# A two-layer graph kernel: gathers issued two blocks ahead with GpSimd's own arithmetic between them, and the first and last loads rearranged

## The chip, the cores and the metric

The kernel runs on one core of a Trainium2 chip. The metric is the time of one execution in device microseconds, as the median of several runs; less is better. Profiles come from one further execution, recorded instruction by instruction.

## The reference

There are 4096 nodes with 512 features each, and an adjacency matrix of 4096 x 4096 int32 values of which about one in a thousand is 1, so a node has some four neighbours. Layer 0 is an eight-head graph attention with a residual and a layer norm; layer 1 takes the mean over the neighbours, two linear maps and a combining one, a relu, a residual and a layer norm.

```python
Wh   = einsum('nf,hfo->hno', x, W)                       # 8 heads of 64
e    = leaky_relu(f1[:, :, None] + f2[:, None, :], 0.2)  # f1, f2: Wh times the halves of a
attn = softmax(where(adj > 0, e, -9e15))
x    = layernorm(x + concat_heads(attn @ Wh))

agg  = (adj > 0) @ x / max(deg, 1)
out  = concat(x @ W_self + b_self, agg @ W_nb + b_nb) @ W_comb + b_comb
x    = layernorm(x + relu(out))
```

## The kernel before

The 4096 rows are handled as 32 blocks of 128. Since the matrix is sparse, the kernel makes lists of neighbours from it and gathers rows instead of multiplying with it. (A dense version stands behind a flag and is not run with these inputs.) The order of instructions on each engine is the order in which the code is written: the schedule is by hand. There are five stages.

**Start.** The weights come in. `fold_weights(1, ...)` multiplies `W_nb` with its half of `W_comb` into `m2` (L265 to L278 and L283), so that layer 1 needs one product per block; VectorE folds the attention vector into `w_sb` (L690, L695). `mask_adj` is a relu on ScalarE (L364) that turns a half block of adjacency into bf16, counts it, and frees its load buffer, of which there are four (`at`).

**Adjacency.** For each block: x is transposed on PE (L301), multiplied with `w_sb` (L309), and the resulting row written to a table `t0` in HBM (L723, the last one L736). `fold_adj`, `max_keys` and, for every four blocks, the generator `decode` turn the adjacency into lists: `idx` holds five row numbers per node, three of its own and two shared slots for nodes with more neighbours, and `es` says to whom the shared ones belong. x is loaded eight blocks ahead and adjacency two blocks ahead on SP's queue.

**First turn.** `gather` (L494) takes the rows of a block with five indirect DMAs issued from GpSimd, into one of `GA = 5` buffers `g`. The first four blocks are gathered at once, twenty DMAs in a row. Meanwhile `fold_weights(0, ...)` makes `m1` from `W_self`, and `split_bias` turns the folded bias into three bf16 rows (`b3`) on VectorE (L251 to L256).

**Attention.** A pipeline over the blocks, one step per block. The softmax of block i+2 (L518 to L549) and the weighting of block i+1 (L562) are on VectorE, the sums over rows on PE (L569, L572, L576), the layer norm of block i on VectorE with its root on GpSimd (`a_moments`, L594), and block i-1 is multiplied with `m2` (L604) and written to the table `t1` (L609). One gather of five DMAs is issued per step, four blocks ahead, after the root.

**Second turn and layer 1.** When `t1` is complete, its rows are gathered in the same way: four blocks at once, and then per block after `g_moments`, when a buffer is free. `g_self` (L620, L623) multiplies a block of x with `m1` and adds the bias; `g_shared` (L627) adds the shared rows on PE; `g_adds` (L614, L615) adds the own ones on VectorE; `g_moments` (L634 to L641) joins them and takes the moments; the square root is on ScalarE (L643) and its reciprocal on VectorE (L646); `g_norm` writes the result (L648, L650, L651).

The order around the second turn, before:

```python
        if i >= NB - 1 and i - NB + 1 < 2:
            g_self(i - NB + 1, transposed(i - NB + 1, wp, "key"), m1)
    G1 = {b: gather(t1, b, gp) for b in range(GA - 1)}
```

Of the kernel before, what the change touches and what calls it, by code (L numbers as in the profile page):

```python
# [39 lines left out]
P = 128  # L40
# [44 lines left out]
def listed_layers(  # L85
# [107 lines left out]
    nc.vector.memset(mhalf, -0.5)  # L193
    eps = const.tile([P, 1], F32, name="eps")
    nc.vector.memset(eps, EPS)
    oner = const.tile([1, P], F32, name="oner")
    nc.vector.memset(oner, 1.0)
    inv_n = const.tile([P, 1], F32, name="inv_n")
    nc.vector.memset(inv_n, 1.0 / N)

# [16 lines left out]
    b3 = const.tile([3, HD], BF16, name="b3")  # L217
    brow = const.tile([1, HD], F32, name="brow")

    tmp_cm.__exit__(None, None, None)  # L220
# [11 lines left out]
    def load_fold(k, w, fp):  # L232
        wr = fp.tile([P, FB, HD], F32, name="wr")
        nc.sync.dma_start(wr, w.rearrange("(c p) o -> p c o", p=P))
        wc = fp.tile([P, FB, HD], F32, name="wc")
        nc.sync.dma_start(
            wc, w_comb[k * HD : (k + 1) * HD, :].rearrange("(c p) o -> p c o", p=P)
        )
        return wr, wc

    def load_bias(k, wp):
        bcol = wp.tile([P, FB], F32, name="bcol", bufs=1)
        with nc.allow_non_contiguous_dma(reason="a vector of 512"):
            nc.scalar.dma_start(bcol, (b_self, b_nb)[k].rearrange("(c p) -> p c", p=P))
        return bcol

    def split_bias(wp):

        bc = wp.tile([P, HD], F32, name="y", bufs=2)[0:1, :]
        nc.scalar.dma_start(bc, b_comb.rearrange("(a o) -> a o", a=1))  # L250
        nc.vector.tensor_add(brow, brow, bc)  # L251
        for k in range(3):
            bb = wp.tile([P, KH * P], F32, name="own", bufs=4)[0:1, :].bitcast(BF16)
            nc.vector.tensor_copy(bb, brow)
            nc.vector.tensor_sub(brow, brow, bb)
            nc.scalar.dma_start(b3[k : k + 1, :], bb)  # L256

    def fold_weights(k, loaded, bcol, m, wp, last=None):

# [11 lines left out]
        for c in range(FB):  # L271
# [8 lines left out]
            yield  # L280
        bp = ps.tile([1, HD], F32, name="nm", bufs=2)
        for d in range(FB):
            nc.tensor.matmul(  # L283
                bp, lhsT=bcol[:, d : d + 1], rhs=wc[:, d, :], start=(d == 0), stop=(d == FB - 1)
            )
        if k == 0:
            nc.vector.tensor_add(brow, brow, bp)
        else:
            nc.vector.tensor_copy(brow, bp)

# [101 lines left out]
    def decode(b0, dp, wp):  # L392
# [46 lines left out]

        sts = []  # L440
        for b in range(b0, b0 + G):
            lt = wp.tile([P, KH * P], F32, name="st", bufs=2)
            nc.vector.tensor_scalar(lt, iota[:, 0 : KH * P], end[:, b : b + 1], None, OP.is_lt)  # L443
            st = wp.tile([P, KH * P], F32, name="own", bufs=4)
            nc.vector.scalar_tensor_tensor(
                st, iota[:, 0 : KH * P], lst[:, b, KL : KL + 1], lt, OP.is_ge, OP.mult
            )
            sts.append(st)
# [41 lines left out]

    def gather(table, b, gp):
        g = gp.tile([P, KS, TW], F32, name="g")
        for k in range(KS):
            nc.gpsimd.indirect_dma_start(  # L494
                out=g[:, k, 0 : table.shape[1]],
                out_offset=None,
                in_=table[:, :],
                in_offset=bass.IndirectOffsetOnAxis(ap=idx[:, b, k : k + 1], axis=0),
            )
        return g  # L500
# [4 lines left out]
    def a_owners(b, wp):  # L505
        OWN[b] = owners(b, wp)
# [74 lines left out]
    def a_two(b, wp):  # L581
        Y[b] = wp.tile([P, HD], F32, name="y", bufs=2)
        nc.vector.tensor_add(Y[b], G0[b][:, 0, H:TW], G0[b][:, 1, H:TW])

# [47 lines left out]
    def g_moments(b):  # L632
# [9 lines left out]
        RS[b] = small.tile([P, 1], F32, name="ln_rs")  # L642
        nc.scalar.activation(RS[b], MV[b][:, 1:2], AF.Sqrt, bias=eps)  # L643

    def g_norm(b, wp):
        nc.vector.reciprocal(RS[b], RS[b])  # L646
        sh = small.tile([P, 1], F32, name="ln_sh")
# [15 lines left out]
    with tc.tile_pool(name="wa", bufs=1) as wa:  # L663
        arow = wa.tile([1, H, 2, D], F32, name="arow")
        nc.scalar.dma_start(arow, a0.rearrange("h (k d) -> h k d", k=2).unsqueeze(0))
        for h in range(H):
            nc.scalar.dma_start(
                w_sb[:, :, H + h * D : H + (h + 1) * D], w0[h].rearrange("(c p) o -> p c o", p=P)
            )
        loaded = load_fold(1, w_nb, wa)  # L670
        load_x(0, xacc)
        load_x(1, xacc)
# [4 lines left out]
        for b in range(4, XL):  # L677
            load_x(b, xacc)
        bcol = load_bias(1, wp)
        pads(wp)  # L680
# [19 lines left out]

        pieces = fold_weights(1, loaded, bcol, m2, wp, first)
        for c in range(FB):
            next(pieces)
            if c >= 2:
                mask_adj(0, c - 2, ap)
        next(pieces, None)
    fp = ctx.enter_context(tc.tile_pool(name="fold", bufs=1))

# [3 lines left out]
    for b in range(NB):  # L712
        load_x(b + XL, xacc)
        load_adj(b + 2, ap)
        if b == NB - 2:
            loaded = load_fold(0, w_self, fp)
            bcol = load_bias(0, wp)
        for p in lists:
# [19 lines left out]
    gp = ctx.enter_context(tc.tile_pool(name="gat", bufs=GA, side="right"))  # L738
    for b in range(GA - 1):
        G0[b] = gather(t0, b, gp)  # L740
    pieces = fold_weights(0, loaded, bcol, m1, wp)
    for k in range(5):
        for p in lists:
            next(p, None)
        next(pieces, None)
    split_bias(wp)
    for b in range(2):
        a_owners(b, wp)

# [4 lines left out]
    for i in range(-2, NB + 2):  # L754
        if on(i):
            a_moments(i)
        if i >= 0 and on(i - 1 + GA):
            G0[i - 1 + GA] = gather(t0, i - 1 + GA, gp)
# [12 lines left out]
        if on(i + 1):  # L771
            a_one(i + 1)
            a_weigh(i + 1, slice(0, 2))
            a_two(i + 1, wp)
        if on(i + 2):
            if i == -2:
                a_owned(0, wp)
                a_owned(1, wp)
            a_shared_sum(i + 2)
            a_sum(i + 2, wp)  # L780
# [4 lines left out]
        if i == -2:  # L785
            continue
        if on(i + 3):
            a_owners(i + 3, wp)
            a_owned(i + 3, wp)
        if i >= NB - 1 and i - NB + 1 < 2:  # L790
            g_self(i - NB + 1, transposed(i - NB + 1, wp, "key"), m1)


    G1 = {b: gather(t1, b, gp) for b in range(GA - 1)}
    for b in range(2):
        OWN[b] = owners(b, wp, scaled=True)
    xT = transposed(2, wp)

# [15 lines left out]
    for b in range(NB + 1):  # L814
        if b + 2 < NB:
            nxt = transposed(b + 3, wp, "key" if b % 2 else "tp") if b + 3 < NB else None
            g_self(b + 2, xT, m1)
            xT = nxt
        if b < NB:
            g_shared(b, G1[b])  # L820
            g_adds(b, G1[b], wp)
        if b > 0:
            g_norm(b - 1, wp)
        if b < NB:
            if b + 2 < NB:
                OWN[b + 2] = owners(b + 2, wp, scaled=True)
            g_moments(b)
            if b + GA - 1 < NB:
                G1[b + GA - 1] = gather(t1, b + GA - 1, gp)
        if b == 4:  # L830
# [397 lines left out]
```

## Time and profile before

| | |
|---|---|
| median of 3 runs | 793.86 us (793.38 to 795.17) |
| the profiled execution | 830.55 us, of which the span from first to last instruction is 828.7 |
| PE busy | 718.1 us (87%) |
| VectorE busy | 556.6 us (67%) |
| GpSimd busy | 427.6 us (52%), of which gathers (L494) 360.0 |
| ScalarE busy | 262.0 us (32%) |
| moved by DMA | 191.28 MB |

Busy shares are averages over stages with different limits, so they say little alone. The page's table of slices cuts the span in 40 equal parts of 20.7 us: a digit is the busy share in tenths, and the row GB/s is what the DMAs moved. The chain that ended last runs back from the last instruction to what released each one. In a timeline a row has its start, its length, the engine, the line of the kernel, the operation with its tiles, and in brackets how long the engine was idle before it and what ended that. In the table of waits a row has who waited for whom, and then microseconds in total, times and the longest. POOL is GpSimd, DVE VectorE, ACT ScalarE, PE the matmul engine, SPq and ACTq the DMA issues of SP and ScalarE. A profiled execution is longer than a timed one here by 36.7 us.

### The profile page before, as it was taken

How to read it: one execution, taken by the hardware profiler on the slowest of the kernel's cores; microseconds unless marked ns; L12 is line 12 of the kernel's file. 1: busy time of each engine (PE TensorE's matmuls, PEld its weight loads, DVE VectorE, ACT ScalarE, POOL GpSimd, SP SyncE). 2: the span in 40 equal slices, each digit the busy share in tenths (PEclk: the TensorE clock that was granted, in tenths of full speed). 3: DMA queues.
4: the chain of work that ended last, by engine and by line, in shares of the span. 5: the costliest groups of instructions: out<-in, count | busy, mean ns of one | idle time of the engine just before them, and what ended most of it. 6: DMA issues, size and time to landing. Idle time of an engine off the chain costs nothing.

```text
span 828.7 us, 9094 instructions
## 1 busy us (share of the span) xinstructions
PE 718.1 (87%) x2806; PEld 386.1 (47%) x2806; DVE 556.6 (67%) x1612; ACT 262.0 (32%) x402; POOL 427.6 (52%) x400
## 2 busy tenths in 40 slices
PE   5998888878997389999999999998937997997983
PEld 2465566656663245555555555543313443443431
DVE  5257787777683588888888888870425684583855
ACT  1576666666641011222222222211201221121311
POOL 3411111210007168888888888602776676676740
PEclk9999999999999599999999999999957998998997
DMA  9899999999956236666656565502775786777751
GB/s 297 292 378 393 392 393 392 393 392 394 391 215 192 66 116 181 196 189 186 197 181 197 181 197 176 167 26 78 218 215 182 212 242 199 223 230 218 227 167 55
DMA packets 85381, 191.28 MB, mean 231 GB/s; under 512 B 13640, under 2 KB 13640, under 8 KB 85326
## 3 DMA queue, kind: packets, MB, share of 16 engines
q0 software_dynamic: 25600, 84.56, 35.1%
q1 hardware_dynamic: 45120, 88.09, 28.6%
q10 hardware_dynamic: 14606, 17.98, 6.2%
q8 instruction: 24, 0.39, 0.2%
q14 instruction: 31, 0.25, 0.1%
HBM read 165.29 MB, written 25.31 MB: 230 GB/s over the span
## 4 chain that ended last, share of the span: by engine, by line
PE 69%; DVE 11%; DMA 7%; issue 6%; another core or an unknown queue 3%; ACT 2%; POOL 0%; ACTq 0%; DVEq 0%; POOLq 0%
PE pw L604 14%; PE pw L309 8%; PE nm L576 7%; PE nm L620 7%; PE pw L620 6%; DMA at<-in_adj_dram 4%; PE nm L572 4%; PE tp L301 3%; PE nm L569 3%; PE pw L275 3%; PE pw L627 3%; PE nm L627 3%; DMA w_sb<-in_L_gnn_W_dram 1%; PE sm L530 1%
## 5 line engine op out<-in xcount | busy, mean ns | idle before, releaser
L494 POOL DMA_INDIRECT g<-t,idx x320 | 360.0, 1125 | 181.7 <-issue 87.4
L364 ACT ACTIVATE ab<-at 128x2048 bf16<-128x2048 int32 x64 | 122.2, 1910 | 63.2 <-DMA at<-in_adj_dram 53.1
L309 PE MATMUL pw<-w_sb,xT 128*128 128x264 f32 x512 | 129.4, 397 | 0.0
L604 PE MATMUL pw<-m,xT 128*128 128x512 f32 x256 | 117.8, 603 | 1.4 <-ACT xT L303 1.4
L295 POOL TENSOR_TENSOR xacc<-xacc,xs 128x512 f32<-128x512 f32 x32 | 41.1, 1284 | 148.1 <-DMA xs<-in_x_dram 147.7
L309 PEld LDWEIGHTS pw<-w_sb,xT 128*128 128x128 f32 x512 | 93.0, 192 | 26.6 <-DVE st L443 3.0
L562 DVE TENSOR_TENSOR g<-g,e 128x1536 f32<-128x1536 f32 x64 | 95.3, 1489 | 1.1
L620 PE MATMUL nm<-m,xT 128*128 128x512 f32 x128 | 65.4, 659 | 22.6 <-ACT xT L303 22.6
L604 PEld LDWEIGHTS pw<-m,xT 128*128 128x128 f32 x256 | 46.0, 190 | 67.0 <-issue 62.0
L620 PE MATMUL pw<-m,xT 128*128 128x512 f32 x128 | 63.5, 642 | 11.9 <-ACT xT L303 11.9
L301 PE MATMUL tp<-ident,xs 128*128 128x128 f32 x320 | 50.1, 279 | 26.1 <-ACT xT L303 26.1
L576 PE MATMUL nm<-g,own 128*128 128x512 f32 x128 | 63.4, 618 | 0.0
L301 PEld LDWEIGHTS tp<-ident,xs 128*128 128x128 f32 x320 | 37.2, 143 | 44.5 <-ACT xT L303 33.3
L643 ACT ACTIVATE ln_rs<-ln_mv,eps 128x1 f32<-128x1 f32 x32 | 9.4, 295 | 150.0 <-DVE ln_mv L641 82.6
L303 ACT COPY xT<-tp 128x512 f32<-128x512 f32 x80 | 46.0, 576 | 23.1 <-PE tp L301 15.9
L313 DVE COPY row<-pw 128x264 f32<-128x264 f32 x64 | 27.3, 426 | 36.2 <-PE pw L309 12.2
L634 DVE SCALAR_TENSOR_TENSOR y<-y,lst,nm 128x512 f32<-128x512 f32 x16 | 11.9, 746 | 57.8 <-remote 32.3
L620 PEld LDWEIGHTS nm<-m,xT 128*128 128x128 f32 x128 | 25.7, 211 | 51.4 <-issue 27.4
L594 POOL TENSOR_TENSOR ln_rs<-ln_rs,mhalf 128x1 f32<-128x1 f32 x32 | 22.7, 710 | 42.9 <-DVE e L555 34.3
L620 PEld LDWEIGHTS pw<-m,xT 128*128 128x128 f32 x128 | 25.2, 207 | 39.9 <-issue 26.7
L587 DVE TENSOR_TENSOR y<-y,nm 128x512 f32<-128x512 f32 x32 | 22.0, 687 | 31.8 <-PE nm L576 30.4
L513 ACT COPY st<-sm 128x256 f32<-128x256 f32 x32 | 11.8, 372 | 94.5 <-PE sm L511 91.4
(166 smaller groups left out, 1015.0 us busy)
## 6 DMA issues: line engine op xcount, KB each, us to landing
at<-in_adj_dram SPq DMA_DIRECT2D x64, 1024.0 KB
t<-row ACTq DMA_DIRECT2D x32, 260.0 KB
xs<-in_x_dram SPq DMA_DIRECT2D x32, 256.0 KB
t<-row ACTq DMA_DIRECT2D x32, 256.0 KB
out_dram<-row SPq DMA_DIRECT2D x32, 256.0 KB
g<-t,idx POOLq DMA_INDIRECT x320
wc<-in_L_gnn_W_comb_dram SPq DMA_DIRECT2D x2, 1024.0 KB
wr<-in_L_gnn_W_nb_dram SPq DMA_DIRECT2D x1, 1024.0 KB
```

Of the source, the lines that this page charges most:

```text
L295: nc.gpsimd.tensor_tensor(xacc, xacc, xs[:, b, :], OP.add)
L301: nc.tensor.transpose(tp[:, c, :], xs[:, b, ts(c, P)], ident)
L303: nc.scalar.copy(t, tp)
L309: nc.tensor.matmul(pw, lhsT=xT[:, c, :], rhs=w_sb[:, c, k * HW : (k + 1) * HW], start=(c == 0), stop=(c == FB - 1),)
L364: nc.scalar.activation(ab, loads.pop((b, h)), AF.Relu, accum_out=asum[:, b, h : h + 1])
L494: nc.gpsimd.indirect_dma_start(out=g[:, k, 0 : table.shape[1]], out_offset=None, in_=table[:, :], in_offset=bass.IndirectOffsetOnAxis(ap=i ...
L562: nc.vector.tensor_tensor(gv, gv, E[b][:, sl].unsqueeze(3).to_broadcast([P, sl.stop - sl.start, H, D]), OP.mult,)
L572: nc.tensor.matmul(NM[b], lhsT=ident, rhs=G0[b][:, 2, H:TW], start=False, stop=False)
L576: nc.tensor.matmul(NM[b], lhsT=OWN[b][:, k, :], rhs=G0[b][:, K0 + k, H:TW], start=False, stop=(k == KH - 1),)
L604: nc.tensor.matmul(pz, lhsT=xT[:, c, :], rhs=m2[:, c, :], start=(c == 0), stop=(c == FB - 1))
L620: nc.tensor.matmul(NM[b], lhsT=xT[:, c, :], rhs=m1[:, c, :], start=(c == 0), stop=False)
L627: nc.tensor.matmul(NM[b], lhsT=OWN[b][:, k, :], rhs=g[:, K0 + k, 0:HD], start=False, stop=(k == KH - 1),)
```

## The change

The gathers at the two turns are issued two blocks ahead instead of four. In the first turn block 2 is gathered after an addition that moves from VectorE to GpSimd for block 0 alone, and blocks 3 and 4 after the root of block 0; from then on there is a gather per step as before. In layer 1 the gather of block b+2 is issued in step b, and the root of block b-1, now a power on GpSimd, stands between its third and fourth DMA.

```diff
+    for b in range(2):
         G0[b] = gather(t0, b, gp)
...
+        if i == 0:
+            G0[3] = gather(t0, 3, gp)
         if i >= 0 and on(i - 1 + GA):
             G0[i - 1 + GA] = gather(t0, i - 1 + GA, gp)
...
-        nc.vector.tensor_add(Y[b], G0[b][:, 0, H:TW], G0[b][:, 1, H:TW])
+        (nc.vector if b else nc.gpsimd).tensor_add(Y[b], G0[b][:, 0, H:TW], G0[b][:, 1, H:TW])
...
             a_two(i + 1, wp)
+            if i == -1:
+                G0[2] = gather(t0, 2, gp)
...
-    def gather(table, b, gp):
+    def gather(table, b, gp, between=None):
         g = gp.tile([P, KS, TW], F32, name="g")
         for k in range(KS):
+            if k == 3 and between:
+                between()
...
+        def root(b=b):
+            if b > 0:
+                nc.gpsimd.tensor_tensor(RS[b - 1], RS[b - 1], mhalf, OP.pow)
         if b < NB:
             g_shared(b, G1[b])
             g_adds(b, G1[b], wp)
+        if b + 2 < NB:
+            G1[b + 2] = gather(t1, b + 2, gp, root)
+        else:
+            root()
...
-            if b + GA - 1 < NB:
-                G1[b + GA - 1] = gather(t1, b + GA - 1, gp)
...
-        nc.scalar.activation(RS[b], MV[b][:, 1:2], AF.Sqrt, bias=eps)
+        nc.vector.tensor_scalar(RS[b], MV[b][:, 1:2], EPS, None, OP.add)
     def g_norm(b, wp):
-        nc.vector.reciprocal(RS[b], RS[b])
```

The order of other work at the turns changes too. In the first turn the owners of blocks 0 and 1 are made and transposed within the weight fold; the last group's `decode` gets one more stop, and its last two parts run in steps -1 and 0 of attention, with their tiles in buffers named `row`; the bias is folded by a function of its own, and its splitting is spread over steps 2, 4, 6 and 8. In the second turn `g_self` of blocks 0 and 1 moves from within the last attention steps to behind the first gathers.

```diff
-    pieces = fold_weights(0, loaded, bcol, m1, wp)
-    for k in range(5):
+    pieces = fold_weights(loaded, m1, wp)
+    for k in range(FB):
         for p in lists:
             next(p, None)
-        next(pieces, None)
-    split_bias(wp)
-    for b in range(2):
-        a_owners(b, wp)
+        next(pieces)
+        if k == 2:
+            for b in range(2):
+                a_owners(b, wp)
+                a_owned(b, wp)
+    next(pieces, None)
+    bias = split_bias(fold_bias(0, loaded, brw), wp)
...
+        if i < 2:
+            for p in lists:
+                next(p, None)
+        elif i % 2 == 0:
+            next(bias, None)
...
-        if i >= NB - 1 and i - NB + 1 < 2:
-            g_self(i - NB + 1, transposed(i - NB + 1, wp, "key"), m1)
-    G1 = {b: gather(t1, b, gp) for b in range(GA - 1)}
+    G1 = {b: gather(t1, b, gp) for b in range(2)}
...
+    xT = transposed(0, wp, "key")
+    for b in range(2):
+        nxt = transposed(b + 1, wp, ("tp", "key")[b])
+        g_self(b, xT, m1)
+        xT = nxt
```

At the start `w_sb` is loaded on SP's queue and `W_nb` with its half of `W_comb` on ScalarE's; the bias vectors are loaded as four rows of 128 and transposed on PE instead of as 512 single words; one constant goes and one is made on ScalarE; and the two relus of block 0 follow pieces 1 and 2 of the weight fold instead of 2 and 3.

```diff
-        nc.sync.dma_start(wr, w.rearrange("(c p) o -> p c o", p=P))
+        (nc.sync, nc.scalar)[k].dma_start(wr, w.rearrange("(c p) o -> p c o", p=P))
...
-            nc.scalar.dma_start(
+            nc.sync.dma_start(
                 w_sb[:, :, H + h * D : H + (h + 1) * D], w0[h].rearrange("(c p) o -> p c o", p=P)
             )
...
-            nc.scalar.dma_start(bcol, (b_self, b_nb)[k].rearrange("(c p) -> p c", p=P))
+        nc.scalar.dma_start(brw, (b_self, b_nb)[k].rearrange("(c p) -> c p", p=P))
...
-            if c >= 2:
-                mask_adj(0, c - 2, ap)
+            if 1 <= c <= 2:
+                mask_adj(0, c - 1, ap)
```

## The prediction

> **What bounds the kernel now.** I read first the page's table of slices. Its GB/s row is low in the first two slices and then flat near 393 from slice 4 to 11: the adjacency stage (about 35 to 243 us) runs at the speed of the DMAs, and its start does not yet. From slice 16 to 27 PE is at 9 throughout: attention. Two holes in PE remain: slice 14, the first turn, and slices 30 and 31, the beginning of layer 1.
>
> ```profile
> PE   5998888878997389999999999998937997997983
> GB/s 297 292 378 393 392 393 392 393 392 394 391 215 192 66 116 181 196 189 186 197 181 197 181 197 176 167 26 78 218 215 182 212 242 199 223 230 218 227 167 55
> ```
>
> Second, the chain that ended last, in order of time. In attention each step is PE after PE, 8.45 us. In the first turn and in layer 1 it names nothing that works:
>
> ```profile
> 259.83 8.44 another core or an unknown queue
> 269.98 6.76 another core or an unknown queue
> 595.89 15.87 issue
> 683.78 9.79 another core or an unknown queue
> ```
>
> Third, the table of waits for 552 to 829 us and the timelines around such a hole. The waiting one is nearly always VectorE's L634, which waits for PE alone (in the first turn L457 and L287, also for PE):
>
> ```profile
> DVE y L634 <- remote: 32.3, 4, 14.0
> DVE y L634 <- PE key L301: 23.6, 2, 15.1
> ```
>
> and in the timeline of PE and VectorE:
>
> ```profile
> 594.32 1.98 PE L627 MATMUL nm<-g,own 128*128 128x512 f32 x4 [0.52 <-issue]
> 609.31 0.75 DVE L634 SCALAR_TENSOR_TENSOR y<-y,lst,nm 128x512 f32<-128x512 f32 x1 [14.03 <-remote]
> ```
>
> L634 needs the L627 group that the record ends at 596.3, and starts at 609.31. So PE's signal arrives 13 us late. Meanwhile GpSimd issues gather after gather, and stalls end where it pauses for want of a free buffer: at 629.05 in a pause of 4.81 us, at 693.60 in one of 2.60. In attention, with a root after every five gathers, there is no such stall. Reading: **PE's signals are held up while GpSimd issues gathers without a break**. The mechanism is not in the trace.
>
> Fourth, GpSimd's timeline: in attention five gathers and a root fill the step, so GpSimd is as full as PE.
>
> ```profile
> 412.69 0.57 POOL L594 TENSOR_TENSOR ln_rs<-ln_rs,mhalf 128x1 f32<-128x1 f32 x1
> 413.43 2.06 POOL L494 DMA_INDIRECT g<-t,idx  x1 [0.17 <-issue]
> 415.80 1.53 POOL L494 DMA_INDIRECT g<-t,idx  x1 [0.30 <-issue]
> ```
>
> **What the Trainium skill says.** "Perfetto Trace Analysis", Summary: the profiler window per engine type: a TensorE end is estimated, signal propagation lies outside every window, and a gather's window is descriptor generation, not the data. The trace agrees: a gather takes 0.95 us, and the second, begun at 573.90, releases VectorE (L614) only at 577.59. So an end of L627 is no proof that its signal was out. "Runtime: NRT & Kernel Launch", Instruction fetch mechanics: code arrives in 16 KiB pages. The trace has 24 such packets (0.39 MB), the nearest to the long stall at 597.4, 12 us before its end: fetching is not the cause. "SBUF — State Buffer", Who interferes with whom: a VectorE op with two SBUF inputs contends with a GpSimd op that reads SBUF. The trace shows 2.06 and 1.53 us for the gathers beside L562, and 0.95 otherwise.
>
> **The change part by part**, against the profiled execution (span 828.7, with 1.85 around it 830.55).
>
> *Start.* ScalarE starts its first copy (L267) at 14.02, held by the issue of w_sb on its queue; L275 at 15.95. w_sb moves to SP's queue ahead of x and adjacency, w_nb and w_comb to ScalarE's, so ScalarE is free when they land: about 3 us sooner, an estimate. Each relu of block 0 moves one piece of the weight fold (3.87) ahead. On SP's queue x and adjacency now stand behind eight w_sb issues; those took 9.71 on ScalarE's queue, and the first adjacency load is issued at 11.04 today, so it hardly moves. The third pair of adjacency loads, waiting for a buffer, was issued at 31.75; now at about 25. The DMAs lose 27 to 42 us at a mean of 250 instead of 392 GB/s, 2.1 MB or 5.4 us. Bounds: 0 (if w_sb ahead on SP delays the first adjacency) and 7 (with the bias read in rows instead of 512 words of 4 B). I take **-5**.
>
> *First turn.* Attention's first matmul (L569) is at 285.9. New order: the fold ends at 259.5, two owner transposes cost 1.1, the bias transpose and copy 0.6, its four matmuls 3.6: 264.8. Softmax of block 0 takes 1.5 (L530 to L549), so L569 is at 266.3: -19.6. Off the path: the bias splitting (4.8, in four portions of some 1.2) goes beside PE's matmuls of later steps, where VectorE is idle 1.3 of 8.45 (7.1 busy); without that cover it costs its 4.8. The last decode (3.3 and 1.7) goes into two early steps, where VectorE waits for block 2's gathers anyway; uncovered, 5. Given back: GpSimd. Block 2's gathers now wait for block 0's addition on GpSimd (1.28, L569+3.8 to +5.1), and blocks 3 and 4 follow root 0 together. Then 5 x 1.28 for block 2, root 0.75, 10 x 1.35: root 1 comes at L569+26.5; before at +16. Since GpSimd has no slack in a step of 8.45, these 10.5 stay, less the 1.5 that a root has before VectorE uses it (412.69 to 414.83): **+9** (5 to 11). Sum of the turn **-10.6**.
>
> *Attention, steady.* Same instructions on each engine: 0. The dropped constant and the one made on ScalarE (0.06 each) lie beside the first loads, the bias loads beside adjacency.
>
> *Second turn.* Block 31's transposes and L604 stood behind block 0's L620:
>
> ```profile
> 560.17 3.70 PE L620 MATMUL nm<-m,xT 128*128 128x512 f32 x8 [1.22 <-ACT xT L303]
> 565.45 3.70 PE L604 MATMUL pw<-m,xT 128*128 128x512 f32 x8 [0.68 <-ACT xT L303]
> 569.81 0.33 ACTq L609 DMA_DIRECT2D t<-row  x1
> 572.60 1.00 POOL L494 DMA_INDIRECT g<-t,idx  x1 [16.34 <-DMA t<-row]
> ```
>
> Without it L604 is at 559.9: **-5.5** (-4 to -6). L620 then runs beside the gathers.
>
> *Layer 1.* From the first gather to the end: 256.1 now. An unbroken run (657.94 to 678.51, 16 gathers) costs 1.286 each, 6.43 per block against PE's 6.1. Without late signals it would be 160 x 1.286 = 205.8, an estimated 4.5 to the last L634 and 9.9 from it to the end (818.8 to 828.7): 220.2. The new root adds 0.51 (0.81 between gathers with a root, 0.30 without), so 6.94. Root 0 comes after 18 gathers, 23.1; root 28 at 23.1 + 28 x 6.94 = 217.4; three more blocks at 3.9, each from a root over L648, owners and moments to the next; from the last moments to the end 7.2 as now: 236.3. Bounds of a root: 0.3 (it fills the gap that every gather has anyway) and 0.75 (0.56 and 0.19 on top of the usual gap): -6 to +7 over 30 blocks. Sum **-19.8**. The wait on a root delays L648, the owners and L634 behind it on VectorE by that much; ScalarE's square root (0.29) and table load (1.28) hide there.
>
> Sum: -5 - 10.6 - 5.5 - 19.8 = **-40.9**: 789.7 by the profiled clock.
>
> **The median.** The timed runs are 793.86, 36.7 below the profiled one. Late signals cost 47.9 in the trace (12.0 in the turn: L287 at 264.8 instead of 276.8; 35.9 in layer 1). If all else costs the same timed, 11.2 of them are left in timed runs and the changed kernel, with none, takes 789.7. Whatever else is cheaper without the profiler comes off. I take 4 of the 36.7 for it: **786**.
>
> **Rivals.** *A, the forecast* (0.43): 786. For it: attention shows that roots between gathers avoid the stalls. *B, slower* (0.26): the late signals exist only under the profiler, which records some 5,600 PE instructions. Then timed: -5 in the start; the turn 266.3 + 9 against 273.9, +1.4; -5.5; layer 1 236.3 against 220.2, +16.1: +7.0, **801**. The mechanism is GpSimd as the bound of layer 1, 6.94 against 6.43. It decides when fewer than 7 us of stall are in the timed runs. Against it: they must have lost 47.9 with only 36.7 to lose. *C* (0.17): the stalls are all real and the 36.7 lies elsewhere: 830.55 - 40.9 - 36.7 = **753**. *D, it doesn't do what it says* (0.14): ten gathers in a row in the turn and 18 in layer 1, as long as what precedes the old stalls; some 6 to 11 us remain, 792 to 797.
>
> **How the numbers follow.** 0.2% is what a measurement here can tell from no change. A and C are faster: 0.60. D is split, 0.08 same and 0.06 slower; with B slower 0.32. Range: 757 leaves out most of C's tail, 810 is B with the start at 0 and a late root (+9). Likeliest case alone: 775 to 792.
>
> **What would show it.** Right: no L634 wait over 5 us and no "remote"; first L569 near 261 (start and turn); first t1 gather about 21 us earlier; GpSimd back to back in layer 1, 6.9 us from root to root, PE with gaps near 0.8 us per step. Wrong: L634 waits of 8 to 15 us between roots (D); a profiled time near 790 with a median above 796 (B); roots waiting for VectorE; adjacency ending no earlier.

## The result and the profile after

The kernel after takes 798.72 us (797.71 to 799.52, four runs) where the kernel before takes 794.51 (793.38 to 795.63, four runs): a ratio of 1.0052 [1.0032, 1.0072], so slower by half a per cent. That rests on four runs of each, all that the kernel after had with signals on time; the kernel before alone takes 784 to 797 in one of the sets of runs below. The forecast was 786 and faster. Rival B had said 801.

The profiled execution of the kernel after took 798.89 us, no longer than its other runs. That of the kernel before had taken 830.55 against 794. The experiments below show why: signals between engines (PE's above all) are late on some chips, in every run as far as its time tells, and on others in none, and the profile of before and its times were of different kinds. Ratios leave out runs over 1.5% above the fastest of their kernel; where signals are late the kernel after spreads from 814 to 837, so that its ratios there are the favourable end (e16's rests on 4 of 22 runs), and medians are given beside them.

The page's table of slices of the kernel after (a slice is 19.9 us), PE and GB/s:

```profile
PE   5997888788999789999999999998999999999972
GB/s 294 363 298 392 392 393 392 392 392 393 393 384 111 97 171 169 192 176 195 195 175 200 193 176 200 190 107 26 172 220 222 235 232 232 232 232 229 230 235 80
```

The hole of slices 30 and 31 is gone: PE is at 9 from slice 29 to 38. The hole in the first turn (slice 14, at 3 before) is at 7. But the third slice of GB/s, 378 before, is now 298.

The table of waits of the kernel after, from 552 us to the end (total, times, longest):

```profile
DVE ln_sh L660 <- POOL ln_rs L846: 66.9, 30, 7.0
...
DVE y L627 <- DMA g<-t,idx: 13.3, 2, 12.9
...
DVE y L647 <- PE nm L640: 5.3, 1, 5.3
```

Of the waits of L647 (the old L634) for PE that one is left, for the first gathers, and there is no "remote". VectorE now waits for GpSimd's root instead, some 2 us in each block. GpSimd's timeline in layer 1, from root to root:

```profile
583.18 0.59 POOL L846 TENSOR_TENSOR ln_rs<-ln_rs,mhalf 128x1 f32<-128x1 f32 x1
583.94 0.99 POOL L506 DMA_INDIRECT g<-t,idx  x1 [0.17 <-issue]
...
587.74 0.95 POOL L506 DMA_INDIRECT g<-t,idx  x1 [0.30 <-DVE y L627]
589.00 0.95 POOL L506 DMA_INDIRECT g<-t,idx  x1 [0.30 <-issue]
589.97 0.59 POOL L846 TENSOR_TENSOR ln_rs<-ln_rs,mhalf 128x1 f32<-128x1 f32 x1
```

6.79 us, and no pause: GpSimd bounds layer 1. In a step of attention, GpSimd's timeline (before, at 412.69, the root took 0.57 and the gather beside L562 2.06):

```profile
414.01 2.07 POOL L607 TENSOR_TENSOR ln_rs<-ln_rs,mhalf 128x1 f32<-128x1 f32 x1
416.26 0.99 POOL L506 DMA_INDIRECT g<-t,idx  x1 [0.18 <-issue]
```

Here the root runs beside VectorE's multiplication (L574, from 413.89) and is stretched to 2.07, while the gather behind it is not: what "SBUF — State Buffer", Who interferes with whom, in the Trainium skill says of the two engines' shared port fits both traces. From root to root it is 8.44 us in both.

At the turns (timelines of the kernel after):

```profile
266.41 1.10 PE L581 MATMUL nm<-xs,ident 128*128 128x512 f32 x2
...
552.84 3.70 PE L617 MATMUL pw<-m,xT 128*128 128x512 f32 x8 [1.22 <-ACT xT L306]
557.19 0.33 ACTq L622 DMA_DIRECT2D t<-row  x1
...
559.98 1.00 POOL L506 DMA_INDIRECT g<-t,idx  x1 [11.06 <-DMA t<-row]
```

Attention's first matmul is at 266.4 instead of 285.9; its last step's product (L617) at 552.8 instead of 565.45; the first gather of `t1` at 559.98 instead of 572.60, which is 12.6 sooner. From there to the end it is 236.8. But the last a_x matmul (L581, before L569, with which a step's sums begin) is only 7.3 sooner, 539.7 instead of 547.0: of the 19.5 won ahead of attention, 12.2 go again in it.

### The profile page after: what moved, and what is told of

It is laid out like the page before. It is cut to its first block, busy times and chain, and to the rows that moved or that the text cites. A ratio compares the mean times of both kernels' runs of the same rounds, so it can differ in the third digit from the quotient of the medians.

```text
span 796.8 us, 9154 instructions
## 1 busy us (share of the span) xinstructions
PE 719.7 (90%) x2808; PEld 381.7 (48%) x2808; DVE 557.7 (70%) x1609; ACT 251.4 (32%) x372; POOL 440.7 (55%) x433
## 3 DMA queue, kind: packets, MB, share of 16 engines
q0 software_dynamic: 25600, 84.56, 36.7%
## 4 chain that ended last, share of the span: by engine, by line
PE 46%; DVE 21%; POOL 13%; DMA 9%; issue 8%; ACT 2%; ACTq 0%; SPq 0%; POOLq 0%; DVEq 0%
PE pw L617 12%; POOL g L506 9%; PE pw L312 7%; PE nm L588 6%; DMA at<-in_adj_dram 4%; PE pw L273 4%; PE nm L584 3%; PE nm L581 3%; PE tp L304 3%; DVE y L627 2%; DVE y L650 2%; DVE ln_bs L653 2%; DVE y L647 2%; POOL ln_rs L846 2%; DMA t<-row 2%
## 5 line engine op out<-in xcount | busy, mean ns | idle before, releaser
L506 POOL DMA_INDIRECT g<-t,idx x320 | 321.1, 1004 | 155.2 <-issue 80.1
L312 PE MATMUL pw<-w_sb,xT 128*128 128x264 f32 x512 | 127.7, 393 | 0.0
L617 PE MATMUL pw<-m,xT 128*128 128x512 f32 x256 | 119.1, 608 | 1.9 <-ACT xT L306 1.9
L312 PEld LDWEIGHTS pw<-w_sb,xT 128*128 128x128 f32 x512 | 92.1, 190 | 26.2 <-issue 3.0
L574 DVE TENSOR_TENSOR g<-g,e 128x1536 f32<-128x1536 f32 x64 | 95.1, 1485 | 1.1
L662 ACT ACTIVATE row<-y,ln_sh,ln_rs 128x512 f32<-128x512 f32 x32 | 26.0, 814 | 175.2 <-issue 143.9
L617 PEld LDWEIGHTS pw<-m,xT 128*128 128x128 f32 x256 | 46.8, 192 | 68.8 <-issue 47.3
L607 POOL TENSOR_TENSOR ln_rs<-ln_rs,mhalf 128x1 f32<-128x1 f32 x32 | 53.9, 1684 | 24.9 <-DVE e L567 16.7
L588 PE MATMUL nm<-g,own 128*128 128x512 f32 x128 | 65.1, 632 | 0.0
L633 PE MATMUL nm<-m,xT 128*128 128x512 f32 x128 | 58.7, 601 | 3.7 <-ACT xT L306 3.4
L633 PE MATMUL pw<-m,xT 128*128 128x512 f32 x128 | 58.8, 602 | 2.4 <-ACT xT L306 2.2
L660 DVE TENSOR_SCALAR ln_sh<-ln_mv,ln_rs 128x1 f32<-128x1 f32 x32 | 6.8, 213 | 66.9 <-POOL ln_rs L846 66.9
L640 PE MATMUL nm<-g,own 128*128 128x512 f32 x64 | 36.3, 666 | 5.4 <-DMA g<-t,idx 5.2
L640 PE MATMUL pw<-g,own 128*128 128x512 f32 x64 | 35.7, 663 | 4.2 <-DMA g<-t,idx 4.0
```

The source lines that it names most:

```text
L312: nc.tensor.matmul(pw, lhsT=xT[:, c, :], rhs=w_sb[:, c, k * HW : (k + 1) * HW], start=(c == 0), stop=(c == FB - 1),)
L506: nc.gpsimd.indirect_dma_start(out=g[:, k, 0 : table.shape[1]], out_offset=None, in_=table[:, :], in_offset=bass.IndirectOffsetOnAxis(ap=i ...
L574: nc.vector.tensor_tensor(gv, gv, E[b][:, sl].unsqueeze(3).to_broadcast([P, sl.stop - sl.start, H, D]), OP.mult,)
L588: nc.tensor.matmul(NM[b], lhsT=OWN[b][:, k, :], rhs=G0[b][:, K0 + k, H:TW], start=False, stop=(k == KH - 1),)
L607: nc.gpsimd.tensor_tensor(RS[b], RS[b], mhalf, OP.pow)
L617: nc.tensor.matmul(pz, lhsT=xT[:, c, :], rhs=m2[:, c, :], start=(c == 0), stop=(c == FB - 1))
```

## The experiments

Besides the change, the kernel after and the kernel before were run again, and each part was undone or done alone. They ran in five sets, each on one chip: e1 to e4 on one numbered 5, e5 to e8 on 11, e9 to e11 on 8, e12 to e15 on 15, e16 to e18 on 13. The kernel before, run beside them, took 827.39 (825.75 to 830.71, 11 runs) on chip 5, 831.45 (35 runs) on 11, **790.55 (784.44 to 796.63, 27 runs) on 8**, 829.73 (33 runs) on 15, 831.84 (827.93 to 839.85, 59 runs) on 13. None of its runs lies between 797 and 825. What is called a chip here may be anything that the runs of a set share. The first runs and profiles have no chip number; a row says "late" or "on time" by what its profile shows.

Two stretches are read from every profile: the time of the first gather of `t1` (start, adjacency, first turn, attention), and from it to the end (layer 1).

| run | chip | first gather of t1 | layer 1 | median | ratio to before |
|---|---|---|---|---|---|
| before, first profile (its times are of the other kind) | late | 572.60 | 256.1 | 794.51 | |
| e5 before | 11, late | 572.36 | 254.3 | 832.40 | 1.0005 [0.9983, 1.0027] |
| e18 before | 13, late | 572.47 | 255.6 | 832.14 | 0.9999 [0.9981, 1.0017] |
| after, first profile | on time | 559.98 | 236.8 | 798.72 | 1.0052 [1.0032, 1.0072] |
| e6 after | 11, late | 560.78 | 272.6 | 833.39 | 0.9944 [0.9908, 0.9980] |
| e12 after | 15, late | 559.31 | 263.5 | 823.59 | 0.9936 [0.9909, 0.9963] |
| e16 after | 13, late | 559.69 | 262.2 | 831.45 | 0.9864 [0.9817, 0.9912] |
| e7 before, layer 1 of after | 11, late | 573.63 | 270.9 | 845.35 | 1.0128 [1.0083, 1.0172] |
| e1 after, layer 1 of before | 5, late | 559.27 | 253.9 | 816.59 | 0.9875 [0.9846, 0.9904] |
| e9 the same | **8, on time** | 559.97 | **224.2** | 787.50 | 0.9964 [0.9944, 0.9985] |
| e2 after, root on ScalarE | 5, late | 559.96 | 252.4 | 814.32 | 0.9857 [0.9830, 0.9884] |
| e15 the same | 15, late | 558.91 | 253.7 | 817.70 | 0.9857 [0.9825, 0.9888] |
| e8 MEMSET for the root | 11, late | 562.95 | 256.2 | 821.77 | 0.9858 [0.9812, 0.9904] |
| e13 turns' order alone | 15, late | 570.00 | 257.7 | 828.24 | 0.9968 [0.9944, 0.9991] |
| e17 the same | 13, late | 573.01 | 255.6 | 829.59 | 0.9957 [0.9937, 0.9977] |
| e14 second turn alone | 15, late | 566.56 | 253.5 | 822.77 | 0.9918 [0.9886, 0.9951] |
| e10 e9 and 256 columns | 8, on time | 559.27 | 258.6 | 816.57 | 1.0323 [1.0274, 1.0372] |
| e11 e9 and 512 columns | 8, on time | 559.92 | 283.5 | 845.08 | 1.0691 [1.0650, 1.0732] |

### Layer 1 undone, and its root undone (e1, e2)

```diff
@@ e1, against after
-        nc.vector.tensor_scalar(RS[b], MV[b][:, 1:2], EPS, None, OP.add)
+        nc.scalar.activation(RS[b], MV[b][:, 1:2], AF.Sqrt, bias=eps)
...
+        nc.vector.reciprocal(RS[b], RS[b])
...
-    G1 = {b: gather(t1, b, gp) for b in range(2)}
+    G1 = {b: gather(t1, b, gp) for b in range(GA - 1)}
...
-        if b + 2 < NB:
-            G1[b + 2] = gather(t1, b + 2, gp, root)
-        else:
-            root()
...
+            if b + GA - 1 < NB:
+                G1[b + GA - 1] = gather(t1, b + GA - 1, gp)
@@ e2, against after (root as in e1)
-            G1[b + 2] = gather(t1, b + 2, gp, root)
-        else:
-            root()
+            G1[b + 2] = gather(t1, b + 2, gp)
```

> The kernel after, with layer 1 alone as in the kernel before: its gathers four blocks ahead and after g_moments, square root on ScalarE, reciprocal on VectorE, no root on GpSimd. Theory B (late PE signals only while a profile is recorded; in timed runs layer 1 is bound by GpSimd, 6.43 us a block without the root and 6.8 to 6.9 with it): timed 783 (779 to 787), some 16 below the 798.7 of the kernel after; profiled 20 to 36 us above its timed time, with L634-like waits of 8 to 15 us. Theory R (a part of the late signals is in timed runs, and that is what the kernel before paid in layer 1): timed 790 to 799. Theory T (the loss is in the first turn, layer 1 costs the same either way): timed 797 to 800.

> The kernel after, with the gathers of layer 1 two blocks ahead as it has them, but the root back on ScalarE and its reciprocal on VectorE, so that nothing stands between the gathers. Theory B: the pace two blocks ahead costs nothing, the root does: timed 783 to 786; in the profile the late signals return and it is 20 us or more longer than timed. Theory R: with gathers unbroken again signals are late in timed runs too: timed 795 to 805. A pacing theory (two blocks ahead is too late for the DMAs, whoever makes the root): timed within 3 us of 798.7.

No theory's figure came out, for a reason that none had: the kernel before took 826 to 831 in all eleven timed runs here. Both kernels were faster than it, 816.59 and 814.32, with late signals in layer 1. The waits of e2:

```profile
DVE y L649 <- remote: 40.2, 3, 20.7
```

Late signals are not an effect of the one profiled execution: theory B in that form fell.

### Both kernels cut before layer 1 (e3, e4)

```diff
-    G1 = {b: gather(t1, b, gp) for b in range(2)}
...
+    nc.sync.dma_start(out[ts(NB - 1, P), :], xs[:, NB - 1, :])
...
-    for b in range(NB + 1):
...
```

> The kernel before without layer 1: it ends when attention is done and the last rows of t1 are written (only one block of the output is stored). Its profile has the stall of the first turn of 12 us. Theory B: the stall is not in timed runs, so timed is about 12 us below its profiled time, near 563. Theory R: timed 566 to 575.

> The kernel after without layer 1, cut at the same place. By its profile the first gather of t1 is at 560.0, so it ends near 562, profiled and timed alike. Theory B: within 2 us of the cut kernel before, timed, so that the whole loss of 4.2 us is in layer 1. Theory R: 3 to 12 us shorter than the cut kernel before. Theory T (the give-back of the first turn is larger in timed runs): 4 us longer or more.

584.7 and 567.3 us: cut like this the kernel after is 17.4 shorter, beyond every theory's figure, and the cut kernel before is far from theory B's 563. Its profiled execution, 584.89, is no longer than its others (584.12 to 588.81): on this chip the stall of the first turn is in all of them. At the first gather of `t1` the traces of the whole kernels differ by 12.6. Most of the rest is an effect of the cut: the cut kernel before still makes `g_self` of block 1 at its very end, some 5.8 us (transposes at 570.07, L620 at 571.89, done at 575.9), and in the cut kernel after that work has gone with layer 1.

### Both kernels again, and layer 1 alone (e5 to e8)

```diff
@@ e7, against before: layer 1 as in the change's diff, nothing else
@@ e8, against after: root as in e1, and
-                nc.gpsimd.tensor_tensor(RS[b - 1], RS[b - 1], mhalf, OP.pow)
+            nc.gpsimd.memset(scr, 0.0)
```

> The kernel before, unchanged, run again. The first time all timed runs took 793 to 796; beside e1 to e4, on a chip that its record numbers 5, eleven took 826 to 831, as its first profiled execution did. Theory S (late PE signals come with the chip, in every run there or in none, and the recording of a profile has no part in it): all runs here, the profiled one too, are of one kind, either 824 to 832 with L634 waits of 8 to 15 us, or 792 to 797 with none over 5 us. Theory B (only the recording makes them): timed 793 to 796 with a profile near 830. If it is 792 to 797 its profile shows what layer 1 costs without late signals: theory B's sum said 220 us from the first gather of t1 to the end, the totals of the two kernels say 231.

> The kernel after, unchanged, run again. Theory S: 797 to 800 whatever the chip, since its trace has no late signals; so 0.96 to 0.97 of the kernel before where that takes 826 to 831, and 1.005 where that takes 794. Theory B: 1.005 on any chip.

> The kernel before with layer 1 alone as in the kernel after (gathers two blocks ahead, root of the block before on GpSimd between the third and fourth). Theory S with late signals: layer 1 falls from 256.1 to 236.8, the stall of the first turn stays: 828 - 19 = 809 (805 to 812). Theory S without late signals: 794.5 plus 236.8 less what layer 1 takes without stalls: 811 if that is 220 (theory B's sum), 800 if it is 231.

> The kernel after with the root of layer 1 back on ScalarE and VectorE, and in its place on GpSimd a MEMSET of one column to a scratch tile (0.10 us each at the start of the kernel). Where late signals occur: if any instruction of GpSimd between gathers releases them, no wait of L634's kind over 5 us and 784 to 792, below the kernel after by the 0.3 to 0.5 us a block that the root costs more; if it takes GpSimd's wait on another engine (the root waits for VectorE, the MEMSET for nothing), stalls as in e2 and 812 to 820. Where they do not occur: 783 to 792.

Chip 11 is of the late kind as well, and theory S's figure for e6 (797 to 800) fell: the kernel after has late signals here in layer 1, 833.39, although its roots stand between the gathers. So **a root between gathers does not keep the signals on time**; the first trace of the kernel after had none, it seems, because it was taken where there are none: e9 below, gathers unbroken, has none there either. A stall of e6 (its profile is of one of its longer executions, 835.46; e12 and e16 have the same stalls; timeline, with the idle time ahead of an instruction and what ended it in brackets):

```profile
596.53 0.96 POOL L506 DMA_INDIRECT g<-t,idx  x1 [0.30 <-issue]
...
600.15 0.60 PE L304 MATMUL tp<-ident,xs 128*128 128x128 f32 x4
600.79 0.75 DVE L647 SCALAR_TENSOR_TENSOR y<-y,lst,nm 128x512 f32<-128x512 f32 x1 [8.74 <-PE tp L304]
...
603.55 0.55 POOL L846 TENSOR_TENSOR ln_rs<-ln_rs,mhalf 128x1 f32<-128x1 f32 x1 [6.07 <-DVE ln_rs L656]
```

VectorE waits 8.74 for PE; GpSimd, which has only two blocks of gathers in store, comes to a root that waits for VectorE and stops for 6.07. In the whole of e6:

```profile
POOL ln_rs L846 <- DVE ln_rs L656: 39.6, 9, 6.1
```

Those 39.6 us are about what layer 1 takes more here than on time, 272.6 less 236.8. In e12 it is 31.0 and 26.7. Without the root a late signal costs less, since GpSimd goes on meanwhile: 252 to 258 in the ten late profiles of a layer 1 without it, whether its gathers are four blocks ahead or two (e2, e15, e8). So it is the root's wait and not the shorter lead. e7 shows the same alone, against its expected 809: before's layer 1 of 254 becomes 271, and the whole 1.3% slower. e8's MEMSETs run within the gap that a gather has anyway (gathers with one between them stay 1.25 apart) and change nothing: 256.2, stalls of up to 20 us, so the theory that any instruction of GpSimd releases the signals fell too.

### On a chip with signals on time: layer 1 of before, and padded gathers (e9 to e11)

```diff
@@ e9: the kernel of e1. e10 and e11, against it:
     def gather(table, b, gp, pad=None):
...
+            if pad is not None:
+                nc.gpsimd.memset(pad, 0.0)
```

> The kernel of e1 again (after with layer 1 as before). Theory S (signals are late in every run on some chips and in none on others): where the kernel before takes 793 to 796 beside it, this one has no wait of L634's kind over 5 us and 783 to 798, which tells what the layer 1 of the kernel after costs there: 783 if an unstalled layer 1 of the kernel before takes 220 us from the first gather, as the prediction summed it; 794 if it takes 232, as the totals say. Where the kernel before takes 826 to 838: 812 to 826, with waits of 8 to 20 us.

> The kernel of e1 with a MEMSET of 256 columns on GpSimd ahead of every gather of layer 1 (a scratch tile, nobody reads it), so that gathers are some 1.4 us apart instead of 1.25. Where signals are late, a rate theory (PE's signals starve when gathers come faster than about one per 1.3 to 1.7 us, as in layer 1, and not in attention with 5 in 8.45): no wait over 5 us, layer 1 of 32 x 7.1 and 15, 800 (795 to 806). A theory of breaks (only a stop of GpSimd of several us lets them through): stalls as in e1, 820 to 835. Where no signal is late: e1's time plus up to 20, if GpSimd alone bounds layer 1.

> As e10, with 512 columns (0.52 us each at the start of the kernel), gathers some 1.65 us apart. Rate theory: no wait over 5 us, layer 1 of 32 x 8.3 and 15, 840 (832 to 848), PE's signals on time throughout; theory of breaks: the stalls stay and come on top, 855 or more. Where no signal is late: 840 as well, bound by GpSimd.

Chip 8 is of the other kind, and e9 came within its 783 to 798. It has the same profiler, the same unbroken gathers, and no "remote" among its waits. The table of waits from 552 us on:

```profile
DVE y L649 <- PE nm L642: 35.7, 16, 5.3
DVE y L649 <- PE pw L642: 28.1, 16, 3.7
```

That is 2 us a block. Its layer 1 is 224.2: from the first gather's begin (559.97) to the last one's (765.83) 1.295 each, 6.47 a block, and 18.4 from there to the end. GpSimd's timeline:

```profile
660.18 0.95 POOL L508 DMA_INDIRECT g<-t,idx  x1 [0.30 <-issue]
661.43 0.95 POOL L508 DMA_INDIRECT g<-t,idx  x1 [0.30 <-issue]
662.68 0.95 POOL L508 DMA_INDIRECT g<-t,idx  x1 [0.30 <-issue]
```

The padded kernels show that GpSimd's pitch is the bound. In e10 a gather comes every 1.523 us on average (559.27 to 801.36), so 160 x 0.228 = 36 more; layer 1 is 34.4 longer, the median 29. In e11 every 1.683: 62 more by this sum, 59.3 in the trace, 57.6 in the median. Both took longer than expected (20 more at most, and 840), e10 because gathers came 1.52 apart and not 1.4. GpSimd's timeline of e10:

```profile
586.93 0.95 POOL L508 DMA_INDIRECT g<-t,idx  x1 [0.17 <-issue]
587.87 0.34 POOL L507 MEMSET z<- 128x256 f32 x1
588.37 0.95 POOL L508 DMA_INDIRECT g<-t,idx  x1 [0.17 <-issue]
```

Beyond the gap of 0.30, nothing hides work on GpSimd here. Against e9, the layer 1 of the kernel after (236.8) costs 12.6 us by the traces: 10.2 up to the last gather's begin (216.1 against 205.9 from the first), 2.4 behind it. By the ratios it is 1.0052 / 0.9964 = 1.0088, some 7 us; runs of e9 spread over 782 to 792, and the two ratios are from two chips, so which figure is nearer is open. No run without the root but with two blocks' lead met a chip with signals on time; that the cost is the root's there is read from GpSimd's timeline, which has no pause. The rate theory of e10 and e11 was not tried where signals are late, since both met a chip where they are not.

### The parts on one chip with late signals (e12 to e15), and once more (e16 to e18)

```diff
@@ e13 and e17, against e1: gathers of the first turn as before
-    for b in range(2):
+    for b in range(GA - 1):
         G0[b] = gather(t0, b, gp)
...
-        if i == 0:
-            G0[3] = gather(t0, 3, gp)
...
-        (nc.vector if b else nc.gpsimd).tensor_add(Y[b], G0[b][:, 0, H:TW], G0[b][:, 1, H:TW])
+        nc.vector.tensor_add(Y[b], G0[b][:, 0, H:TW], G0[b][:, 1, H:TW])
...
-            if i == -1:
-                G0[2] = gather(t0, 2, gp)
@@ e14, against before: g_self of blocks 0 and 1 behind the first gathers of t1, as in the change's diff
```

> The kernel after, unchanged, beside the others of this call. Where the kernel before takes 784 to 797 (signals on time): 1.003 to 1.008 of it, as the first time. Where it takes 826 to 838 (signals late): 0.985 to 1.005 of it, with waits of 5 to 9 us, as in e6.

> The kernel after with layer 1 as before (e1) and also the gathers of the first turn as before: four blocks at once, one more per step, block 0's addition on VectorE. What is left of the change is the order of the turns' other work and of the start. Signals on time: the give-back of the first turn goes (9 by the prediction's sum, about 7 by the traces: L617 of block 31 at 552.8 where the sum of the parts gives 546), so 7 to 9 below e9: 776 to 784, the fastest of all. A theory in which the give-back is small: within 3 us of e9. Signals late: the stall of about 12 us in the first turn returns: 8 to 14 above e1, 822 to 832.

> The kernel before with g_self of blocks 0 and 1 moved behind the first gathers of t1, nothing else. By the prediction 5.5 us sooner (4 to 6), whether signals are late or not: 0.993 of the kernel before. If those products then hold up layer 1's first blocks: 0.997 to 1.0.

> The kernel of e2 again (gathers of layer 1 two blocks ahead, no root on GpSimd). Signals on time: the root's 12.6 us of e9's trace against the trace of the kernel after comes off whole, if the pace of two blocks ahead costs nothing: e12 less 10 to 13. If the pace costs, 0 to 8 less. Signals late: 0.98 to 0.99 of the kernel before, as e2.

Chips 15 and 13 are of the late kind, so what these runs say is of that kind. The second turn alone (e14) gives 5.9 us in the trace (566.56 against 572.5) and 7.0 in the median, with 5.5 predicted: the one part whose gain came out. Without the root (e15) the kernel is 5.9 us below the kernel after of the same chip. With four blocks gathered at once in the first turn (e13) the stall is back there, and 10.7 us with it (570.00 against 559.31); the waits of e13 and of e18 in the first turn:

```profile
DVE dn L556 <- remote: 11.4, 1, 11.4
```

```profile
DVE es L457 <- remote: 13.5, 1, 13.5
```

Ten gathers in a row and then a stop, as the kernel after has them in the first turn, left no such wait in e6, e12 or e16.

e13 shows one thing more. It has the four blocks of gathers in store, and GpSimd stands idle before its first root, yet its first steps of attention are as long as those of the kernel after. From the first a_x matmul to the fifth it takes 46.3 us, e17 45.4, the kernel after 44.4, the kernel before 32.7; the later steps agree. So the lost time does not need the two blocks' lead. In the kernel after the first two steps take 10.0 and 15.3 us instead of 6.5 and 9.3, most of the 11.7; they are those that now carry the last two parts of `decode` (L448 to L483), whose chain goes from VectorE to PE and back. GpSimd's timeline of e13, and VectorE's of the kernel after:

```profile
288.68 0.58 POOL L609 TENSOR_TENSOR ln_rs<-ln_rs,mhalf 128x1 f32<-128x1 f32 x1 [15.46 <-DVE ln_rs L608]
```

```profile
288.29 0.36 DVE L467 COPY es<-sm 128x192 f32<-128x192 f32 x1 [4.43 <-PE sm L463]
```

e13 differs from e14, on the same chip, by the start and the other work of the first turn, without the new order of gathers: 570.00 against 566.56, and 828.24 against 822.77 in the median. So that part of the change loses 3 to 5 us there. No run puts `decode` back alone.

> The kernel after, unchanged, beside e17 and e18. Signals on time (the kernel before at 784 to 797): 1.003 to 1.008 of the kernel before; its first gather of t1 at 560, 6.8 us a block in layer 1. Signals late (826 to 838): 0.99 to 1.0 of it, as e6 and e12.

> The kernel of e13 again: of the change only the start and the order of the turns' other work, gathers as before. Signals on time: no stall in the first turn, the first gather of t1 at 551 to 554 instead of 560, layer 1 of 224 as in e9: 776 to 784, 0.985 of the kernel before (0.980 to 0.992) and the fastest. If the first turn's pacing gave nothing back: 0.996, as e9. Signals late: 0.997, as e13.

> The kernel before again, for its profile. Signals on time: no wait of L634's kind over 5.5 us, L287 at 264 to 265 instead of 276.8 and the first L569 near 273.9, as the prediction summed it without the late signals; the first gather of t1 near 560.6, from it to the end 224 as in e9, so a span near 785 to 790. Signals late: as e5.

Late again: 831.45 for the kernel after (814.48 to 836.08; by medians 0.9995 of the kernel before), 829.59 and 832.14. What e13's kernel does where signals are on time, and a profile of the kernel before there, stay open.

By these ratios the kernel of e1 and e9 (the change without its layer 1) is below the kernel before on either kind of chip, and by medians below the kernel after as well, though they never ran beside each other: 0.9964 of the kernel before where signals are on time and the kernel after has 1.0052, 0.9875 where they are late and the kernel after has 0.986 to 0.994 by ratios and 0.993 to 1.002 by medians (e1 0.987 by medians).

## Why the prediction was wrong

**The step that failed is "The median".** It put 32.7 of the 36.7 us between the profiled execution and the timed runs down to stalls that recording had caused, and held that the rest of its 47.9 us of late signals was in every timed run, for the change to win back. The profiled executions of the kernel after (798.89) and of e9 (785.93) are no longer than their other runs, so recording costs nothing here; and 138 runs of the kernel before beside e1 to e8 and e12 to e18, all between 825 and 840, with the stalls in the profiles of e5 and e18, show that late signals are in timed runs too, where the chip has them. So the 36.7 was the difference between two kinds of execution. The times to be predicted were of the kind without late signals; of the stalls there was next to nothing to gain. The 47.9 was too large as well: 35.9 of it lay in layer 1, where e9, on time, leaves 256.1 - 224.2 = 31.9; so the sum that had to leave 11.2 in the timed runs was no sign that they held any. Rival B had the right outcome with a wrong cause, "only under the profiler", and its right mechanism in layer 1, GpSimd as the bound. That its 801 came so near is in part luck: start and turns gave 6.3 us less than it had them give, layer 1 cost 3.5 to 9 less, and the two errors cancel (the figures are below).

**The reading that a root between gathers keeps signals on time** fell in layer 1 (e6, e12, e16). What held is that a break does, in the first turn, where the gathers stop after ten (e13 against e12). In the three profiles of before, 16 of the 18 waits of L634 over 5 us for PE or "remote" do end in a pause of GpSimd, as the prediction said; but the one of 14.03 us that it showed ends at 609.31, amid gathers begun at 608.07 and 609.33. In attention, where a step has a root and slower gathers, no trace has such a stall. Whether the stop or the lower rate matters is open.

Term by term, against traces:

- *Start*, predicted -5: 0. The last product of the adjacency stage (L312, before L309) begins at 239.52 instead of 239.58. The third pair of adjacency loads was indeed issued sooner, 27.65 instead of 31.75, but the hole moved to the next. The table of stretches (PE, PEld, DVE, ACT and POOL busy, PE clock, DMA share, GB/s), first of before, then of after:

```profile
30.00:35.00 5.00, 5.00 (x13) 1.46 (x12) 0.00 (x0) 4.09 (x5) 4.69 (x5) 1.00 0.35 129
```

```profile
40.00:45.00 5.00, 5.00 (x40) 3.58 (x32) 2.01 (x9) 4.37 (x5) 0.00 (x0) 1.00 0.18 59
```

The second load of the next pair is issued only at about 42.3, when block 1's second relu has freed a buffer; that relu waits until 40.35 for a product on PE (L379) that stands behind the fold, and PE ends the fold at 37.2 (before at 36.6). The sum did not ask what was late next. ScalarE was not freed either: its first copy waited until 14.79 for its own queue, by the record for the load of `brw`:

```profile
14.79 1.07 ACT L265 COPY xT<-nm 128x512 f32<-128x512 f32 x2 [11.92 <-DMA brw<-in_L_gnn_b_nb_dram]
```

- *First turn*, predicted -10.6, as -19.6 and +9 given back. The first came out: 285.9 to 266.4. But from the first to the last a_x matmul attention takes 273.3 (266.4 to 539.7) instead of 261.1 (285.9 to 547.0), so the give-back is **12.2**, above its range. Nor does it need the cause that was stated, GpSimd's late start: root 1 does come 25.8 after the first a_x matmul (26.5 predicted), but VectorE's L606, for which it waits, ends just then too, and e13 and e17 lose as much with the gathers of before. By the steps that grew, the term that failed is the last `decode`, put at nothing, or 5 if not hidden. The first matmul was won by putting work behind it. And the -19.6 is against a kernel before that stalls; on time it should be less, but no profile of that is at hand.
- *Second turn*, predicted -5.5: of the 12.6 at the first gather of `t1`, 7.3 are there at the last a_x matmul, so 5.3; e14 alone 5.9.
- *Layer 1*, predicted 236.3: 236.8. The unstalled layer 1 of before was put at 220.2: e9 has 224.2, of which 206.8 are to the end of the last gather (205.8 predicted) and 17.4 from there to the end (14.4 predicted). So rival B's +16.1 is +12.6 by the traces. Root to root was predicted 6.94 and is 6.79, so a root of 0.59 adds 0.32 to e9's 6.47 and not 0.51.

For chips with signals on time B's sum (-5, +1.4, -5.5, +16.1 = +7.0) becomes: start and turns together -2.8 (e9's 0.9964 of 790.55, its layer 1 being that of before), predicted -9.1; layer 1 +7 to +12.6; measured in all +4.2. That is the second thing that the forecast had wrong: even without any late signal the start and turns give less than summed, and the root, though it costs less too, outweighs them.

Where signals are late, the forecast's larger figure (-40.9) fell as well: the turns give the 12.6 of the trace, and layer 1 takes 7 to 18 us back (262 to 273 against 254 to 256), because a late signal now stops GpSimd too.

## What to carry to other kernels

Before a profile's stalls are priced, ask whether its own time agrees with the times to be predicted; a profiled execution 4.6% longer was here of another kind, and the sum of its stalls no gain. Where one engine issues all the gathers and is full, arithmetic on it is paid for all but what fits into the gaps (0.32 of 0.59 us here), and putting it among the gathers makes the gathers wait for whatever the arithmetic waits for. Work moved behind a milestone makes the milestone early and not the end: price it where it lands. When a load is moved ahead, look for the next one in the same queue: a hole in the DMAs moves on to it unless what frees its buffer moves too.

## What the runs showed of the hardware

- One kernel, unchanged, takes 784 to 797 us on some chips and 825 to 840 on others. On the latter, while GpSimd issues gathers 1.25 us apart, VectorE waits up to 27.1 us for signals of PE, and ScalarE up to 8.5 (e7). The longest, in e5's layer 1:

```profile
DVE y L634 <- remote: 60.7, 7, 27.1
```

  GpSimd's gathers take 0.95 us and gaps of 0.30 on both kinds, and the granted clock differs little (0.95 to 0.96 against 0.97 to 0.98 over a run of the kernel before). The lower clock does not start a stall: in the first profile of before it is still full from 595 to 600 us, when PE's signals are already missing. The table of stretches:

```profile
595.00:600.00 5.00, 5.00 (x16) 2.29 (x14) 0.28 (x1) 0.89 (x2) 3.78 (x5) 1.00 0.76 214
605.00:610.00 5.00, 0.51 (x3) 0.11 (x1) 0.69 (x1) 0.00 (x0) 3.78 (x5) 0.50 0.70 207
```

  What makes the difference between chips was not found.
- It is the signals that are late, and not PE's alone. The traces also keep the times at which each engine raised its semaphores. In the four profiles on time (after, e9 to e11) each of PE's 584 raises lies within 0.06 us of the end of its matmul. In the first profile of before that holds up to the first gather (195 raises); from there on only 323 of 394 raises of PE are in the record, 681 of 888 of VectorE and 136 of 231 of ScalarE, and some come long after: the bias product (L283) ends at 264.75, and the raise that lets L287 go stands at 276.75. In e6 no raise of PE stands between 590.76 and 600.68, and then there are eight within 0.39 us, where the record has eight ends of PE from 583.89 to 600.75; GpSimd's last gather before them had ended at 597.49. Whether the missing ones were merged or only not recorded is open.
- A MEMSET of one column between two gathers (0.12 us, e8) costs nothing, one of 256 columns (0.33, e10) makes the pitch 1.44 where the gather itself takes 0.95: it starts as the gather before it ends, and the gather behind it has a gap of 0.17 and not 0.30.
